# Layer 1 of a two-layer convolutional attention: one shift in 16 goes from VectorE to GpSimd, and the weights of each unit's last two chunks are summed by TensorE

## The chip, the cores and the metric

The kernel runs on one core of a Trainium2 chip. A core has TensorE (PE; its weight loads are listed as PEld), VectorE (DVE), ScalarE (ACT), GpSimd (POOL) and SyncE (SP, which issues most DMAs). Each works through its own queue in order and waits on semaphores for the others. The metric is the device time of one launch in microseconds, the median of the runs; the times of single instructions come from one profiled execution.

## The reference, cut to what matters

`x` is 2 x 256 x 64 x 64, so two images of 256 channels and N = 4096 places. Layer 0 is an attention with four heads of 16 channels and is not touched here. Layer 1 is an attention with four heads of 64 channels:

```python
def _L1_conv_ref(x, w_qkv, b_qkv, w_out, b_out):
    ...
    qkv = jnp.einsum('oc,bchw->bohw', w_qkv, x) + b_qkv[None, :, None, None]
    qkv = qkv.reshape(b, HEADS, 3 * head_dim, h * w)
    q, k, v = jnp.split(qkv, 3, axis=2)
    scale = 1.0 / jnp.sqrt(jnp.asarray(head_dim, x.dtype))
    attn = jax.nn.softmax(jnp.einsum('bhdn,bhdm->bhnm', q, k) * scale, axis=-1)
    out = jnp.einsum('bhnm,bhdm->bhnd', attn, v).reshape(b, c, h, w)
    return jnp.einsum('oc,bchw->bohw', w_out, out) + b_out[None, :, None, None] + x
```

All is in 32-bit floats. Each softmax needs, for a query, the maximum over 4096 keys, the exps of the shifted scores, their sum, and their product with v.

## The kernel before

**Units, chunks and groups.** Layer 1 is cut into 32 units: an image, a pair of heads, and 512 queries. A unit's 4096 keys are 32 chunks of 128 (`NM`), and a chunk's tile is 128 keys x (2 heads x 512 queries), 128x1024. The chunks form two groups of 16 (`GS`, `NG`), each with a maximum of its own; the groups are put together at the end by a factor.

**What happens to a chunk.** `score` makes the scores on TensorE (L876) in PSUM; two buffers, `pair`, take turns. `keep` takes them into the group's running maximum on VectorE (L893), then copies them to SBUF on ScalarE (L894) as the tile `raw`, from a ring of 26. When a group has all its scores, `turn_max` transposes the maxima (L906), `fold` reduces them to one negated maximum a query (L923) and sends them through DRAM, so that they come back as `row`, the same values in all 128 partitions (L926, L930). In `row` a head's queries stand in an order in which two neighbours belong to different halves of a block, so it is read with every second element. `place_shift` has ScalarE copy `row`, put in order, into a PSUM tile (L943). Then, chunk by chunk, `shift` adds that to `raw` on VectorE (L951), and `weigh` takes the exp on ScalarE (L963) and has GpSimd add the weights to the group's `acc` (L973 for the first two chunks of a group, L975 for each later one). `gather` multiplies the weights with v on TensorE (L1004).

**Sums.** `acc` has still 128 keys to be added up. `total` does it on TensorE with a matrix of ones (L1026): a result of 32 equal rows for each group and head, at rows 0, 32, 64 and 96 of the PSUM tile `misc`. That tile has one buffer, which the projections of keys, values and queries and all transposes use in turn. `keep_total` copies the sums out on ScalarE (L1034).

**Order.** It is written out by hand: `seq` keeps instructions in program order on each engine. A step handles two chunks, 16 steps make a unit (`US`), and a chunk's shift comes `LAG` = 11 steps after its scores, so the end of a unit overlaps with the next one. Step t has these parts in this order:

- scores of chunks 2t and 2t+1; `weigh` of chunk 2t-23; what is hung at "start" and "early"
- `keep` of 2t, `shift` and `weigh` of 2t-22; what is hung at "early end"
- `keep` of 2t+1, `gather` of 2t-24 and 2t-23; "late" and "late end"; `shift` of 2t-21; "end"

`at(t, place, ...)` hangs the rest between. Counted in a unit's own steps 0 to 15: the maxima are turned in step 8 and, for the second group, in step 0 of the next unit. `place_shift` comes at the end of step 10, and of step 2 of the next unit. The weights of chunks 30 and 31 are gathered in step 11 of the next unit, whose "early" part projects half of the queries of the unit after into `misc`, which ScalarE reads at "early end" (L858). `total` follows in step 12. Chunk 6 of a unit is shifted in its step 14, chunk 22 in step 6 of the next one.

**The last unit.** From chunk `LATE` on, weights are summed on TensorE already in half of the steps (`on_tensor`, `late_sums`, L990), since nothing follows that would cover GpSimd.

Of the kernel before, what the change touches and what calls it, by code (L numbers as in the profile page):

```python
# [10 lines left out]
ALU = mybir.AluOpType  # L11
# [3 lines left out]
P = 128  # L15
# [5 lines left out]
D1 = 64  # L21
# [5 lines left out]
def conv_attention_kernel(  # L27
# [19 lines left out]
    nc = tc.nc  # L47
    B, _, N = x.shape
    NJ = N // NB
    NM = N // P  # L50
# [75 lines left out]
    for s in range(3):  # L126
        t = const_prep.tile([P, CC, P], F32, tag=f"wpad{s}", name=f"wpad{s}")
# [27 lines left out]
    for i in range(2):  # L155
        t = const0.tile([P, PB, P], F32, tag=f"negmax0_{i}", name=f"negmax0_{i}")
# [20 lines left out]
    def layer1_constants():  # L177

        w1 = const.tile([P, CC, 3, C], F32, tag="w1", name="w1")
        for c in range(CC):  # L180
            for k in range(3):
                later_load(
                    w1[:, c, k, :].rearrange("p (h d) -> p h d", d=D1),
                    w_qkvT[c * P : (c + 1) * P, :].rearrange(
                        "p (h t d) -> p t h d", t=3, d=D1
                    )[:, k],
                )
        wo1 = later_load(
            const.tile([P, CC, C], F32, tag="wo1", name="wo1"), w_outT.rearrange(by_chunk, p=P)
        )  # L190

        b1 = const.tile([P, PR, 3], F32, tag="b1", name="b1")
        for k in range(2):
            later_load(
                b1[k * D1 : (k + 1) * D1],
                b_qkv_col.rearrange("d (g k t) -> d g k t", k=2, t=3)[:, :, k, :],
            )
        b1v = later_load(
            const.tile([P, H, D1], F32, tag="b1v", name="b1v"),
            b_qkv_row.rearrange("(h t d) -> t h d", t=3, d=D1)[2].partition_broadcast(P),  # L200
        )
        bo1 = later_load(const.tile([P, CC], F32, tag="bo1", name="bo1"), b_out)
        ones = const.tile([P, D1], F32, tag="ones", name="ones")
        nc.gpsimd.memset(ones, 1.0)
        return w1, wo1, b1, b1v, bo1, ones


    seq = tc.keep_in_program_order
# [24 lines left out]
    with own0:  # L233
# [189 lines left out]
        def weigh(t, g):  # L423
            u = b, j = units0[t // NM]
            m = t % NM
            pt = l0w.tile([P, 2, NB], F32, tag="p", bufs=4, name=f"p0_{b}_{j}_{m}_{g}")
            for k in range(2):
                h = 2 * g + k
                r = slice(32 * h, 32 * h + 32)

                late = 4 * (t + LEAD0 - END0) + h
                if late >= 0 and late % 7 < 4:
                    ps = bank(f"s0_{b}_{j}_{m}_{h}")
                else:
                    ps = ps2.tile([P, NB], F32, tag="s", name=f"s0_{b}_{j}_{m}_{h}")
                seq(nc.tensor.matmul(  # L436
                    ps, kTs[b][r, bass.ts(m, P)], qs0[u][r, :], start=True, stop=True
                ))
                seq(nc.scalar.activation(pt[:, k, :], ps, AF.Exp, scale=D0**-0.5))  # L439
            pts[t, g] = pt  # L440
# [205 lines left out]
        w1, wo1, b1, b1v, bo1, ones = layer1_constants()  # L646
# [4 lines left out]
        def misc(name):  # L651
            return small_bank[0](name)
# [57 lines left out]
        for i in range(NJ):  # L710
            k = (0, 0, i)
# [17 lines left out]
        for t in range(-LEAD0 + NM, max(t for t, _ in extras) + 1):  # L729
            ahead = t + LEAD0  # L730
            whole = ahead >= END0
            hung(t, "start")
            if 0 <= t < END0:
                weigh(t, 0)
            if ahead < END0:
                maxima(ahead, 1)
            if 0 <= t - 1 < END0 and not whole:
                gather(t - 1, 0)
            hung(t, "middle")
            if 0 <= t < END0:  # L740
                weigh(t, 1)
            if ahead < END0:
                maxima(ahead, 0)
            if 0 <= t - 1 < END0:
                gather(t - 1, None if whole else 1)
            hung(t, "end")
# [12 lines left out]
    units = [(b, g, j) for b in range(B) for g in range(PR) for j in range(NJ)]  # L759
    GS = NM // 2  # L760
    NG = NM // GS
# [2 lines left out]
    END = len(units) * US  # L764


    LATE = len(units) * NM - 2 * LAG
    with (
        tc.tile_pool(name="l1", bufs=2) as l1,
# [7 lines left out]
        rmax, negs, rows_in, shifts, raws, accs = {}, {}, {}, {}, {}, {}  # L777
        avs1, srows, losts, joined, halves = {}, {}, {}, {}, {}
# [160 lines left out]
        def place_shift(u, n):  # L939
            b, g, j = u  # L940
            ps = psb.tile([P, 2, NB], F32, tag="shift", name=f"shift_{b}_{g}_{j}_{n}")
            row = rows_in.pop((u, n))
            seq(nc.scalar.copy(  # L943
                ps.rearrange("p k (a i m) -> p (k a) i m", m=P, i=2),
                row.rearrange("p k (a m i) -> p (k a) i m", m=P, i=2),
            ))
            shifts[u, n] = ps

        def shift(t):
            u = units[t // NM]  # L950
            seq(nc.vector.tensor_tensor(  # L951
                raws[t], raws[t], shifts[u, t % NM // GS], ALU.add
            ))

        def on_tensor(t):
            return t >= LATE and (t // 2 % 2 == 1 or t == 2 * END - 3)

        def weigh(t):
            u = b, g, j = units[t // NM]
            m = t % NM  # L960
            n = m // GS
            p = raws[t]
            seq(nc.scalar.activation(p, p, AF.Exp, scale=D1**-0.5))  # L963

            if on_tensor(t):
                return
            if (u, n) not in first:
                first[u, n] = p
            elif (u, n) not in accs:
                accs[u, n] = l1.tile(  # L970
                    [P, 2, NB], F32, tag="acc", bufs=3, name=f"acc_{b}_{g}_{j}_{n}"
                )
                seq(nc.gpsimd.tensor_tensor(accs[u, n], first[u, n], p, ALU.add))  # L973
            else:
                seq(nc.gpsimd.tensor_tensor(accs[u, n], accs[u, n], p, ALU.add))  # L975

        def late_sums(of):


            if "sums" not in late:  # L980
                late["sums"] = psp.tile([P, 2, NB], F32, tag="pair", name="late_sums")
            t = of[1] if of[1] is not None else of[0]
            u, n = (units[t // NM], t % NM // GS) if t is not None else (units[-1], 0)
            for k in range(2):
                for i in range(2):
                    if of[i] is None and (i == 1 or n == 1 and t != 2 * END - 3):
                        continue
                    p = raws[of[i]] if of[i] is not None else accs[u, n]
                    r = D1 * i + 32 * k
                    seq(nc.tensor.matmul(  # L990
                        late["sums"][r : r + 32, n, :], ones[:, :32], p[:, k, :],
                        start=(n, r) not in begun, stop=True, skip_group_check=True,
                    ))
                    begun.add((n, r))

        def gather(t):
            u = b, g, j = units[t // NM]
            m = t % NM
            n = m // GS
            if m % GS == 0:  # L1000
                avs1[u, n] = psv.tile([P, NB], F32, tag="av", name=f"av1_{b}_{g}_{j}_{n}")
            v = vs[b, g, m // PB]
            for k in range(2):
                seq(nc.tensor.matmul(  # L1004
                    avs1[u, n][k * D1 : (k + 1) * D1, :], v[:, m % PB, k, :], raws[t][:, k, :],
                    start=(m % GS == 0), stop=(m % GS == GS - 1),
                ))
            if on_tensor(t) and t % 2 == 1 and t != 2 * END - 1:
                late_sums((t - 1, t) if on_tensor(t - 1) else (None, t))
            elif t == 2 * END - 2:  # L1010
                late_sums((t, t + 1))
            raws.pop(t - 2, None)
            if m % GS == GS - 1:
                a = l1.tile([P, NB], F32, tag="avs", name=f"avs1_{b}_{g}_{j}_{n}")
                seq(nc.scalar.copy(a, avs1.pop((u, n))))
                avs1[u, n] = a

        def total(u):


            b, g, j = u
            srows[u] = misc(f"sum1_{b}_{g}_{j}")
            for n in range(NG):
                for k in range(2):
                    r = D1 * n + 32 * k
                    seq(nc.tensor.matmul(  # L1026
                        srows[u][r : r + 32, :], ones[:, :32], accs[u, n][:, k, :],
                        start=True, stop=True,
                    ))

        def keep_total(u):
# [161 lines left out]
        for n, u in enumerate(units):  # L1193
            b, g, j = u
# [231 lines left out]
```

## Time and profile before

| | |
|---|---|
| Median of 3 runs | 4668.57 us (4666.47 to 4668.93) |
| Profiled execution | 4667.5 us |
| Its span | 4665.7 us |
| Granted TensorE clock in it, mean | 0.997 |
| Layer 0, and the change to layer 1 | about the first 2060 us |
| One unit of layer 1, start to start | 79.8 us in units 3 to 23, 79.9 later |

A line of the page's list of groups names the source line, engine and operation, then output<-inputs, the shapes and the count; after the bar come the group's busy time in us and the mean of one in ns, and after the second bar how long the engine stood idle before such instructions, and what ended that. A line of a timeline gives the start, the length (several equal instructions in a row are merged, x8), and in brackets an idle time before it. Durations of neighbours overlap a little: VectorE's operations on 128x1024 last 1.21 us but start 1.13 us apart. A TensorE matmul of 32-bit floats appears as two passes, so that the four matmuls of `gather` are x8.

### The profile page before, as it was taken

The page shows a single profiled execution, that of the slowest core. Times are in us where ns is not written, and L with a number is a line of the kernel's source. Part 1 is how long each engine was busy: PE and PEld are TensorE (multiplying, and loading weights), DVE is VectorE, ACT ScalarE, POOL GpSimd, SP SyncE. Part 2 cuts the span into 40 slices and gives each one's busy share as a digit, 9 for nine tenths or more (in the row PEclk, how much of TensorE's full clock was granted, in tenths as well). Part 3 has the DMA queues.
Part 4 walks back from the last instruction along what each step waited for, and adds up shares of the span by engine and source line. Part 5 has one row for each costly group of instructions (what it writes and reads, how often), then busy time and mean ns, then how long its engine had stood idle before and what let it go on. Part 6 is the DMA issues. An engine that isn't in the chain of part 4 may idle for free. (4 is left out here: it accounts for less than half of the span.)

```text
span 4665.7 us, 70910 instructions
## 1 busy us (share of the span) xinstructions
PE 4496.5 (96%) x27290; PEld 1511.0 (32%) x27290; DVE 3894.2 (83%) x4506; ACT 3429.5 (74%) x4588; POOL 2513.9 (54%) x1306
## 2 busy tenths in 40 slices
PE   8999999999999999999999999999999999999998
PEld 3433333333333333332333333333333333222232
DVE  6777777777777777439999999999999999999997
ACT  3366666666666666668888888888888888888885
POOL 5300000000000000009999999999999999999995
PEclk9999999999999999999999999999999999999999
DMA  3100000000000000121111221111211112121213
GB/s 100 39 4 20 20 20 15 15 15 15 15 17 15 15 13 13 40 77 35 35 37 33 63 48 42 35 37 43 69 41 39 37 33 62 48 53 37 53 39 111
DMA packets 199682, 174.70 MB, mean 37 GB/s; under 512 B 121256, under 2 KB 122088, under 8 KB 199344
## 3 DMA queue, kind: packets, MB, share of 16 engines
q1 hardware_dynamic: 197488, 169.58, 13.9%
q8 instruction: 214, 3.51, 0.3%
q14 instruction: 124, 1.02, 0.1%
q10 hardware_dynamic: 1856, 0.59, 0.1%
HBM read 127.65 MB, written 42.48 MB: 36 GB/s over the span
## 5 line engine op out<-in xcount | busy, mean ns | idle before, releaser
L975 POOL TENSOR_TENSOR acc<-acc,raw 128x1024 f32<-128x1024 f32 x883 | 2095.2, 2373 | 82.3 <-ACT raw L963 21.1
L402 DVE TENSOR_REDUCE mx<-a 128x1 f32<-128x512 f32 x2048 | 1314.4, 685 | 449.7 <-PE a L398 448.7
L439 ACT ACTIVATE p<-s 128x512 f32<-128x512 f32 x2048 | 1107.8, 595 | 702.1 <-PE a L398 369.3
L876 PE MATMUL s<-q,k 64*128 64x512 f32 x4096 | 1120.9, 637 | 126.1 <-ACT raw L894 117.9
L951 DVE TENSOR_TENSOR raw<-raw,shift 128x1024 f32<-128x1024 f32 x1024 | 1234.2, 1209 | 3.9 <-ACT shift L943 2.6
L893 DVE TENSOR_TENSOR rmax<-s,rmax 128x1024 f32<-128x1024 f32 x960 | 1168.7, 1217 | 74.4 <-PE s L876 68.3
L436 PE MATMUL s<-q,kT 32*128 32x512 f32 x4096 | 1218.0, 640 | 0.0
L894 ACT COPY raw<-s 128x1024 f32<-128x1024 f32 x1024 | 1034.2, 1010 | 207.3 <-DVE rmax L893 162.0
L963 ACT ACTIVATE raw<-raw 128x1024 f32<-128x1024 f32 x1024 | 1084.8, 1060 | 133.6 <-DVE raw L951 101.2
L398 PE MATMUL a<-kT,q 32*128 32x512 f32 x4096 | 1129.3, 643 | 1.4 <-DVE mx L402 1.3
L1004 PE MATMUL av<-raw,v 128*64 128x512 f32 x4096 | 992.8, 605 | 3.5 <-ACT raw L963 3.4
L451 PE MATMUL av<-p,v 128*32 128x256 f32 (+1 forms) x7904 | 650.1, 399 | 0.6 <-ACT avs L465 0.6
L876 PEld LDWEIGHTS s<-q,k 64*128 64x128 f32 x4096 | 314.6, 185 | 858.5 <-ACT raw L894 600.9
L501 POOL TENSOR_TENSOR f<-f,dyn 128x16 f32<-128x16 f32 x15 | 3.3, 221 | 1027.3 <-DVE f L500 1027.3
L436 PEld LDWEIGHTS s<-q,kT 32*128 32x128 f32 x4096 | 397.2, 183 | 425.8 <-issue 392.6
L451 PEld LDWEIGHTS av<-p,v 128*32 128x32 f32 x7904 | 157.7, 108 | 751.4 <-issue 737.1
L1004 PEld LDWEIGHTS av<-raw,v 128*64 128x64 f32 x4096 | 247.7, 136 | 468.8 <-issue 350.1
L552 POOL TENSOR_SCALAR res<-res 128x1024 f32<-128x1024 f32 x16 | 16.7, 1045 | 659.6 <-ACT res L551 659.6
L398 PEld LDWEIGHTS a<-kT,q 32*128 32x128 f32 x4096 | 305.1, 183 | 31.5 <-DVE mx L402 18.2
L973 POOL TENSOR_TENSOR acc<-raw,raw 128x1024 f32<-128x1024 f32 x64 | 152.6, 2385 | 124.2 <-ACT raw L963 124.2
L923 DVE TENSOR_REDUCE negs<-rt 128x4 f32<-128x512 f32 x126 | 86.7, 688 | 50.4 <-PE rt L906 50.4
L306 DVE RECIPROCAL std<-std 128x128 f32<-128x128 f32 x64 | 56.1, 920 | 39.5 <-ACT std L301 39.5
(335 smaller groups left out, 1835.1 us busy)
## 6 DMA issues: line engine op xcount, KB each, us to landing
row<-neg SPq DMA_DIRECT2D x128, 256.0 KB
x<-in_x_dram SPq DMA_DIRECT2D x16, 512.0 KB
res<-in_x_dram SPq DMA_DIRECT2D x16, 512.0 KB
x<-res SPq DMA_DIRECT2D x16, 512.0 KB
att<-rows SPq DMA_DIRECT2D x62, 128.0 KB
kd<-k1s SPq DMA_DIRECT2D x24, 256.0 KB
vd<-v1s SPq DMA_DIRECT2D x24, 256.0 KB
k<-kd SPq DMA_DIRECT2D x24, 256.0 KB
```

Source lines behind the costliest of these rows:

```text
L398: seq(nc.tensor.matmul(ps, qs0[u][r, bass.ts(i, P)], kTs[b][r, bass.ts(m, NB)], start=True, stop=True,))
L402: seq(nc.vector.tensor_reduce(mxs[u][:, i * H + h, m : m + 1], ps, AX.X, ALU.max))
L436: seq(nc.tensor.matmul(ps, kTs[b][r, bass.ts(m, P)], qs0[u][r, :], start=True, stop=True))
L439: seq(nc.scalar.activation(pt[:, k, :], ps, AF.Exp, scale=D0**-0.5))
L451: seq(nc.tensor.matmul(avs[u][32 * h : 32 * h + 32, cols], vs0[b][:, m, 32 * h : 32 * h + 32], pts[t, h // 2][:, h % 2, cols], start=(m == ...
L876: seq(nc.tensor.matmul(ps[:, k, :], ks[b, g, m // PB][r, bass.ts(m % PB, P)], qs1[u][r, :], start=True, stop=True,))
L893: seq(nc.vector.tensor_tensor(rmax[u, n], ps, before, ALU.max))
L894: seq(nc.scalar.copy(raw, ps))
L951: seq(nc.vector.tensor_tensor(raws[t], raws[t], shifts[u, t % NM // GS], ALU.add))
L963: seq(nc.scalar.activation(p, p, AF.Exp, scale=D1**-0.5))
L975: seq(nc.gpsimd.tensor_tensor(accs[u, n], accs[u, n], p, ALU.add))
L1004: seq(nc.tensor.matmul(avs1[u, n][k * D1 : (k + 1) * D1, :], v[:, m % PB, k, :], raws[t][:, k, :], start=(m % GS == 0), stop=(m % GS == GS ...
```

## The change

One chunk of each group, the one with the number 6 in it (chunks 6 and 22 of a unit), is shifted by GpSimd instead of VectorE. GpSimd reads `row` itself, with every second element, since the ordered copy is in PSUM; the addition stands in GpSimd's queue where `place_shift` is called, four steps before the chunk's turn. The last group of the last unit is left out. In exchange GpSimd no longer adds chunks 30 and 31 of a unit to `acc` (except in the last unit, where TensorE has these already). Their sums are made on TensorE from the weights themselves, right behind their `gather`, and land in rows 64 to 127 of the tile that `total` completes a step later; so `misc` is taken one step earlier, and `total` adds the second group's `acc` to what is there.

```diff
+    ALSO = 6
...
             shifts[u, n] = ps
+            if (u, n) != (units[-1], NG - 1):
+                a = raws[units.index(u) * NM + n * GS + ALSO]
+                seq(nc.gpsimd.tensor_tensor(
+                    a.rearrange("p k (a i m) -> p (k a) i m", m=P, i=2),
+                    a.rearrange("p k (a i m) -> p (k a) i m", m=P, i=2),
+                    row.rearrange("p k (a m i) -> p (k a) i m", m=P, i=2),
+                    ALU.add,
+                ))
 
         def shift(t):
             u = units[t // NM]
+            if t % GS == ALSO and t < (len(units) - 1) * NM + GS:
+                return
             seq(nc.vector.tensor_tensor(
                 raws[t], raws[t], shifts[u, t % NM // GS], ALU.add
             ))
...
-            if on_tensor(t):
+            if on_tensor(t) or m >= NM - 2:
                 return
...
                 late_sums((t, t + 1))
+            if m == NM - 1 and u != units[-1]:
+                srows[u] = misc(f"sum1_{b}_{g}_{j}")
+                for i in (t - 1, t):
+                    for k in range(2):
+                        r = D1 * (NG - 1) + 32 * k
+                        seq(nc.tensor.matmul(
+                            srows[u][r : r + 32, :], ones[:, :32], raws[i][:, k, :],
+                            start=(i < t), stop=False, skip_group_check=True,
+                        ))
...
             b, g, j = u
-            srows[u] = misc(f"sum1_{b}_{g}_{j}")
             for n in range(NG):
                 for k in range(2):
                     r = D1 * n + 32 * k
                     seq(nc.tensor.matmul(
                         srows[u][r : r + 32, :], ones[:, :32], accs[u, n][:, k, :],
-                        start=True, stop=True,
+                        start=(n < NG - 1), stop=True, skip_group_check=True,
                     ))
```

## The prediction

> **What bounds the kernel now.** The change lies in layer 1, the second half of the span, so I read the page's totals and costliest groups first.
>
> ```profile
> PE 4496.5 (96%) x27290; PEld 1511.0 (32%) x27290; DVE 3894.2 (83%) x4506; ACT 3429.5 (74%) x4588; POOL 2513.9 (54%) x1306
> L975 POOL TENSOR_TENSOR acc<-acc,raw 128x1024 f32<-128x1024 f32 x883 | 2095.2, 2373 | 82.3 <-ACT raw L963 21.1
> L951 DVE TENSOR_TENSOR raw<-raw,shift 128x1024 f32<-128x1024 f32 x1024 | 1234.2, 1209 | 3.9 <-ACT shift L943 2.6
> L893 DVE TENSOR_TENSOR rmax<-s,rmax 128x1024 f32<-128x1024 f32 x960 | 1168.7, 1217 | 74.4 <-PE s L876 68.3
> L943 ACT COPY shift<-row 128x1024 f32<-128x1024 f32 x64 | 71.2, 1113 | 3.8 <-DMA row<-neg 1.5
> ```
>
> These shares mix two layers. One unit of layer 1 repeats every 79.8 us, and the table by stretches shows one such period:
>
> ```profile
> 2974.80:3054.60 79.80, 75.73 (x324) 24.77 (x322) 75.98 (x71) 69.51 (x76) 74.23 (x37) 1.00 0.17 37
> ```
>
> After the length come PE, PEld, DVE, ACT and POOL. PE, DVE and POOL are each busy 93 to 95%, so totals don't say which sets the pace; each place of the change has to be read. First the waits from 2200 to 4600 us (sum, times, longest):
>
> ```profile
> DVE rmax L893 <- PE s L876: 62.3, 149, 0.9
> PE s L876 <- ACT raw L894: 105.3, 211, 0.9
> POOL acc L973 <- ACT raw L963: 74.9, 60, 2.1
> ```
>
> DVE waits for scores; PE waits for a score buffer that ACT empties. Now PE's timeline around the place where the new matmuls go (step 11 of the following unit: the av x8 at 2973.84 are chunks 30 and 31, the sums at 2978.02 are step 12):
>
> ```profile
> 2972.78 1.13 PE L806 MATMUL q1p<-b_('q', (0, 1, 4))_24637,w 128*128 128x256 f32 x4
> 2973.84 1.94 PE L1004 MATMUL av<-raw,v 128*64 128x512 f32 x8
> 2975.71 2.38 PE L876 MATMUL s<-q,k 64*128 64x512 f32 x8
> 2978.02 1.07 PE L1026 MATMUL sum<-acc,ones 128*32 128x512 f32 x8
> 2979.02 1.94 PE L1004 MATMUL av<-raw,v 128*64 128x512 f32 x8
> 2988.39 1.94 PE L1004 MATMUL av<-raw,v 128*64 128x512 f32 x8
> 2990.26 2.28 PE L876 MATMUL s<-q,k 64*128 64x512 f32 x8
> ```
>
> From 2970.74 to past 2992 each PE group starts as the one before ends. DVE in the same stretch, and at step 6:
>
> ```profile
> 2976.89 1.22 DVE L893 TENSOR_TENSOR rmax<-s,rmax 128x1024 f32<-128x1024 f32 x1 [0.36 <-PE s L876]
> 2987.79 1.21 DVE L951 TENSOR_TENSOR raw<-raw,shift 128x1024 f32<-128x1024 f32 x1
> 2991.43 1.22 DVE L893 TENSOR_TENSOR rmax<-s,rmax 128x1024 f32<-128x1024 f32 x1
> 3031.74 1.22 DVE L893 TENSOR_TENSOR rmax<-s,rmax 128x1024 f32<-128x1024 f32 x1 [0.58 <-PE s L876]
> ```
>
> DVE waits for PE there, not PE for DVE. Last, ACT's read of the bank that the new sums need, and POOL where the second group's shift goes in:
>
> ```profile
> 2975.55 0.47 ACT L858 ACTIVATE q<-q1p,b 128x256 f32<-128x256 f32 x1
> 3010.71 7.28 POOL L975 TENSOR_TENSOR acc<-acc,raw 128x1024 f32<-128x1024 f32 x3
> 3018.75 2.39 POOL L973 TENSOR_TENSOR acc<-raw,raw 128x1024 f32<-128x1024 f32 x1 [0.77 <-ACT raw L963]
> ```
>
> **PE, added: 31 units, 4 matmuls (8 traced passes) each.** They follow the av of step 11, where the next group could start at 2975.71. They write the misc bank, which has one buffer, and ACT reads the queries out of it until 2975.55+0.47=2976.02; the wait is about 0.3 us. The passes use two of the array's column ranges (rows 64 and 96 of the result), four passes each. Two rows price that: av, also 8 passes on two ranges, 2973.84 to 2975.71, 1.87; the present sums, 8 passes on four ranges, 2978.02 to 2979.02, so 2 passes a range in 1.00 and 4 in 2.00. I take 1.94. Against it: the two score chunks of step 12 start 1.25 apart where back to back is 1.06, a wait for a buffer that will be over, 0.19. Part of that comes back, because the later chunk's copy and the next scores are late by the full amount. Net 2.05 to 2.25, taken 2.15 us a unit; 31 x 2.15 = 66.7 us.
>
> The Trainium skill (TensorEngine Tiling (Array Packing), Theoretical Speedup) gives up to 4x for a small dimension of at most 32, which would make the 8 passes 1.00 us and the sum some 29 us less. The trace shows that speed where four ranges are written; two are written here.
>
> Does anything downstream take the delay in? From 2976 to 2992 PE has only one other gap, about 0.1 before chunk 29, and it waits for a copy that is late too. The larger gaps after (0.61 at 2996.07, the two around L1051 and L876 up to 0.57) end with DVE or ACT work that follows these very scores. I count nothing back.
>
> **DVE, removed: 63 shifts.** Their spacing is 1.13 (2987.79 to 2988.91), so 71.2 us of DVE. Chunk 6 is the one at 2987.79, in step 14. Without it, the maximum of chunk 29 moves up by about 1.0, then the next shift; but the maximum of chunk 30 at 2991.43 needs scores that PE begins at 2990.26 behind its av of 2988.39, and that order doesn't move. Chunk 22 is at 3027.69, in step 6; the following maximum at 3031.74 already waits 0.58 for PE, which runs without a gap from 3026.99 to 3036.12. Both cuts lengthen a DVE wait: 0. If that cover were gone, each would give up to 1.13.
>
> **POOL, swapped: 62 additions out, 63 shifts in.** Out: 62 x 2.373 = 147.1. In: no row of POOL at this size reads every second element, as the shift does of `row`. Below: the plain 2.373 (149.5 in all). Nothing makes it cheaper, since it has the elements of an addition. Above: ACT's copy of the same `row` takes 1113 against 1010 ns plain, 1.10 times, so 2.61 (164.6). Far end, an estimate: if POOL pays for the stretch that it reads, one of its two inputs counts double, 1.5 x 2.373 = 3.56. I take 2.4, the same operation with one input changed, with ACT's row as the nearest sign of a surcharge. The Trainium skill (GPSIMD Engine Reference, Performance pitfalls for Q7 kernels) puts 50% on reads with a step of more than 8 bytes; this step is 8 bytes, so the rule lets the plain price hold. No row here shows it.
>
> Place of the first group's shift: behind chunk 29's addition, ahead of the next group's first, before which POOL idles 2.1 us and where an addition of chunks 30 and 31 each has gone. It costs nothing, even if a row comes late. Place of the second: between the additions of chunks 14 and 15. Chunk 14's ends about 3015.5, the shift runs to 3018.0, chunk 15's to 3020.4 (before: 3017.99), then chunks 16 and 17 start 1.6 late. Queued behind chunk 15's addition is a buffer: ACT's copy of chunk 9 of the next unit, at 3020.67, goes into the slot that it frees. The margin is 0.3 at 2.373 and nil at 2.61. Beyond that each 0.1 costs up to 0.1 a unit. Later additions had 3 to 5 us to their slot's reuse and keep 1.4 or more; the two dropped ones at the unit's end give the 1.6 back. `row` is landed: ACT read it from 3012.38 on, and of 64 reads two waited. The two exps that now wait for POOL come four steps after. SP's next write of `row`, 6 steps on, now waits for POOL too, 20 us past its read. 0 us.
>
> **Sum.** The profiled execution is 4667.5 us (span 4665.7 and 1.8 around it), 1.1 under the median of 4668.57. 4667.5+66.7 = 4734.2; on the median's footing 4735.
>
> **Rivals.** (A) PE pays, and a cut shift counts: if one of the two lay on the path, 31 x 1.13 = 35 back, 4700; if the passes overlapped as the present sums do, 1.00 for 8 and not 1.94, 31 x 0.94 = 29 less, 4706. Against: the waits named above. Chance 0.09. (B) Faster: the period is DVE's. It's busy 76.0 of 79.8, PE has 4.1 idle to take 2.15 in, and the 71.2 count: 4597. For: DVE has the largest sum. It decides if PE's recorded ends are late enough that PE has over 2 us of true slack in steps 11 to 14; against: the maxima start within 0.05 of the scores' recorded ends. Chance 0.08; that both count in full (-4.5, 4664, no change) 0.03. (C) The strided shift outgrows POOL's margin: at the far end of 3.56, chunk 15's addition ends 1.2 later than with 2.373, 0.9 past the margin, and ACT's copy with it; with 0.2 for POOL's later start 31 x 1.1 = 34 more, 4769. For: the copy at 3020.67 is followed at once by the scores that need its buffer. Against: ACT's own surcharge is 0.1. Chance 0.12. The forecast, 4730 to 4740 by its own terms, 0.68. That the swap isn't made is excluded by the program's order: POOL has one 128x1024 operation more.
>
> **Numbers.** Range 4700 to 4770: it takes in A and C's bounds, and leaves B and no change out. About 0.2% (9 us) is what a measurement tells from no change. Faster 0.08, same 0.03, slower 0.89.
>
> **What would show it.** Right: period near 82.0; new matmuls 1.9 behind an 0.3 wait on L858; DVE's wait for scores (62.3) grown by over 100; shifts on POOL near 2.4, ACT's copies not waiting on POOL. Wrong: a period of 77 to 80, PE's waits for ACT shrunk; or copies released by POOL.

## The result and the profile after

The changed kernel takes 4721.89 us (4721.34 to 4722.56, 4 runs) beside 4668.19 for the kernel before: 1.0116 times, 95% interval 1.0098 to 1.0133, or 53.7 us more where 66.7 were forecast. It is inside the range, on the side that was forecast, and a fifth smaller than the sum; it lies under the 4730 to 4740 that the forecast gave by its own terms.

The profiled execution has a span of 4719.6 us. One period of layer 1 in the table by stretches (length, then PE, PEld, DVE, ACT and POOL busy):

```profile
2934.80:3016.40 81.60, 77.20 (x330) 25.26 (x328) 73.98 (x69) 69.12 (x76) 74.08 (x37) 1.00 0.16 36
```

The period grew from 79.8 to 81.6 us. PE gained 1.5 us of work, DVE lost 2.0 and POOL lost 0.15; which of these moved the time, the steps below and the runs tell. The waits from 2200 to 4600 us:

```profile
DVE rmax L896 <- PE s L879: 170.4, 234, 2.7
PE s L879 <- ACT raw L897: 110.5, 263, 0.9
PE sum L1030 <- ACT q L861: 7.6, 29, 0.3
```

DVE's wait for scores went from 62.3 to 170.4 us. That holds both what was cut from DVE and the longer period: with the new sums alone (the first run below) it is 125.8.

One row of these waits looks like the sign that the prediction named for being wrong: ACT's copies of scores are put down to POOL's small operation on `sums` (L1138), 29 times, 16.4 us. But that copy starts 1.31 us after the start of its own maximum on DVE (3006.38 to 3007.69), just as the copies next to it do (3001.43 to 3002.74, 3010.80 to 3012.11), so by this spacing it is the maximum that releases it. And the row is the same, 29 times and 16.4 us, in the run where GpSimd shifts nothing, so the moved shift isn't behind it.

PE's timeline around the new matmuls (L1030), for the same unit as before:

```profile
2991.40 1.94 PE L1017 MATMUL av<-raw,v 128*64 128x512 f32 x8
2993.63 1.91 PE L1030 MATMUL sum<-raw,ones 128*32 128x512 f32 x8 [0.29 <-ACT q L861]
2995.47 1.99 PE L879 MATMUL s<-q,k 64*128 64x512 f32 x8
2997.39 1.07 PE L1047 MATMUL sum<-acc,ones 128*32 128x512 f32 x8
2998.38 1.94 PE L1017 MATMUL av<-raw,v 128*64 128x512 f32 x8
3000.25 1.13 PE L879 MATMUL s<-q,k 64*128 64x512 f32 x4
3001.64 1.13 PE L879 MATMUL s<-q,k 64*128 64x512 f32 x4 [0.27 <-ACT raw L897]
```

The wait for the `misc` bank is there, 0.29 us, and the 8 passes take 1.84 us up to the next start. DVE and POOL at the places of the change:

```profile
2996.64 1.23 DVE L896 TENSOR_TENSOR rmax<-s,rmax 128x1024 f32<-128x1024 f32 x1 [2.56 <-PE s L879]
3010.80 1.23 DVE L896 TENSOR_TENSOR rmax<-s,rmax 128x1024 f32<-128x1024 f32 x1 [0.63 <-PE s L879]
```

```profile
2989.67 2.43 POOL L953 TENSOR_TENSOR raw<-raw,row 128x1024 f32<-128x1024 f32 x1
2995.99 2.37 POOL L986 TENSOR_TENSOR acc<-raw,raw 128x1024 f32<-128x1024 f32 x1 [3.90 <-ACT raw L976]
3034.86 2.41 POOL L953 TENSOR_TENSOR raw<-raw,row 128x1024 f32<-128x1024 f32 x1
```

The first group's shift lies in POOL's idle time with 3.9 us to spare, and the shift costs 2.41.

**The same by steps.** The trace gives the start of every score copy on ScalarE; the spacing of the even chunks' copies is the length of a step. Means over seven units in the middle (8 to 14), in us:

```
                     step 1     2     6     9    11    12    13    14   period
before                 5.72  5.34  5.20  4.52  4.53  5.14  4.58  4.79    79.81
changed                5.74  5.33  5.19  4.52  6.70  4.78  4.96  4.42    81.64
```

Steps 0 to 10 are unchanged, step 6 with its cut shift among them. Step 11, with the new matmuls, is 2.17 longer; steps 12 to 14 give 0.36 back, take 0.38 and give 0.37. The net is 1.82 a period. Some periods of before were longer than 79.8 for other waits, so all 31 together grew by 53.3.

### The profile page after: what moved, and what is told of

Same layout as the page of the kernel before. It is cut to its first block, busy times and chain, and to the rows that moved or that the text cites. A ratio compares the mean times of both kernels' runs of the same rounds, so it can differ in the third digit from the quotient of the medians.

```text
span 4719.6 us, 71331 instructions
## 1 busy us (share of the span) xinstructions
PE 4542.9 (96%) x27538; PEld 1526.2 (32%) x27538; DVE 3832.3 (81%) x4443; ACT 3418.6 (72%) x4588; POOL 2512.0 (53%) x1307
## 5 line engine op out<-in xcount | busy, mean ns | idle before, releaser
L988 POOL TENSOR_TENSOR acc<-acc,raw 128x1024 f32<-128x1024 f32 x821 | 1948.0, 2373 | 115.8 <-ACT raw L976 65.2
L879 PE MATMUL s<-q,k 64*128 64x512 f32 x4096 | 1107.7, 634 | 126.5 <-ACT raw L897 124.8
L964 DVE TENSOR_TENSOR raw<-raw,shift 128x1024 f32<-128x1024 f32 x961 | 1159.9, 1211 | 2.8 <-ACT shift L946 1.5
L953 POOL TENSOR_TENSOR raw<-raw,row 128x1024 f32<-128x1024 f32 x63 | 151.8, 2409 | 36.0 <-DMA row<-neg 36.0
```

The lines of the kernel that those rows point to most:

```text
L879: seq(nc.tensor.matmul(ps[:, k, :], ks[b, g, m // PB][r, bass.ts(m % PB, P)], qs1[u][r, :], start=True, stop=True,))
L964: seq(nc.vector.tensor_tensor(raws[t], raws[t], shifts[u, t % NM // GS], ALU.add))
```

## The experiments

The runs were on several chips, on which the kernel before took 4668 to 4681 us; each is compared by its ratio to the kernel before on its own chip. Verdicts rest on ratios and on the step table. Steps that an edit doesn't reach agree to 0.02 us between chips, but for step 2 (more on it below):

```
                     step 1     2     6     9    11    12    13    14   period   last 7
before                 5.72  5.34  5.20  4.52  4.53  5.14  4.58  4.79    79.81    79.88
sums only              5.72  5.72  5.19  4.52  6.70  4.78  4.96  4.59    82.17    82.17
6 and 22 unshifted     5.74  5.68  5.19  4.53  4.53  5.15  4.56  4.81    80.19    80.20
12 and 28 unshifted    5.06  6.15  5.19  3.93  4.57  5.12  4.63  4.74    79.40    79.92
12 and 28 on GpSimd    5.06  6.51  5.19  3.92  6.71  4.78  4.96  4.59    81.86    81.50
changed, again         5.74  5.43  5.19  4.53  6.70  4.78  4.96  4.42    81.74    81.82
four ranges            5.74  5.40  5.19  4.52  5.85  4.78  4.96  4.42    80.87    81.04
28 unshifted           5.72  5.43  5.19  3.92  4.57  5.12  4.64  4.74    79.33    79.90
28 on GpSimd           5.72  5.36  5.19  3.92  4.58  5.12  4.64  4.74    79.27    81.20
28, first 24 units     5.72  5.57  5.19  3.92  4.57  5.11  4.64  4.74    79.45    80.25
```

The last column is the mean period from unit 24 on.

**The sums alone.** The changed kernel without the shift on GpSimd:

```diff
-            if (u, n) != (units[-1], NG - 1):
-                a = raws[units.index(u) * NM + n * GS + ALSO]
-                seq(nc.gpsimd.tensor_tensor(
...
-                ))
...
-            if t % GS == ALSO and t < (len(units) - 1) * NM + GS:
-                return
```

> VectorE shifts every chunk again; GpSimd still drops the additions of chunks 30 and 31 and TensorE makes their sums. Theory (the cut shifts are worth nothing, the sums on TensorE's path are the whole loss): the time of the changed kernel, 4717 to 4727 us. Rival (a cut shift gave back part, and what is seen is a net): the recovery of about 0.35 us a unit seen in step 14 is the cut's, 31 x 0.35 = 11 more, 4733; if a whole shift counted, 31 x 1.13 = 35 more, 4757.

It takes 1.0126 times the kernel before (1.0111 to 1.0141), 61.3 us more. Beside the changed kernel's 1.0115 and 1.0116 that leaves 0.1%, some 5 us, for the shift on GpSimd; the intervals of the ratios overlap, but the step table shows where it lies: step 14 is 4.59 here and 4.42 in the changed kernel, in each unit, 31 x 0.17 = 5.3. So neither answer was right as put: the sums cost 1.99 us a unit (steps 11 to 14 together 21.03 against 19.04), and the cut in step 14 pays 0.17 of it back. The reason is in ScalarE's queue. In the run with the sums alone, VectorE's shift of chunk 6 ends at 3098.26, and only then can ScalarE take its exp (first line). The copy of chunk 29 stands behind that exp, and TensorE waits 0.40 for it before the scores of chunk 31 (second line):

```profile
3098.29 1.06 ACT L966 ACTIVATE raw<-raw 128x1024 f32<-128x1024 f32 x1
3100.67 1.13 PE L879 MATMUL s<-q,k 64*128 64x512 f32 x4 [0.40 <-ACT raw L897]
```

In the changed kernel the exp starts 0.91 after the copy of chunk 28 does, instead of 1.07, and the same scores wait 0.23:

```profile
3010.98 1.13 PE L879 MATMUL s<-q,k 64*128 64x512 f32 x4 [0.23 <-ACT raw L897]
```

**No one shifts chunks 6 and 22.** Kernel before, with

```diff
         def shift(t):
             u = units[t // NM]
+            if t % GS == 6 and t < (len(units) - 1) * NM + GS:
+                return
```

> The kernel before, but nobody shifts chunks 6 and 22 of a unit (they stay unshifted, the last group apart); sums as before. Theory (VectorE waits for TensorE in steps 6 and 14): 4664 to 4670, no change. Rival (VectorE sets the period): 63 x 1.13 = 71 less, 4597; half of it, 4633.

It takes 4681.44 us beside 4681.27: 0.9997 (0.9987 to 1.0006). 71 us of VectorE's work were taken away with nothing in exchange, and the time didn't move; by the interval it fell by 6 us at most. The work turned into waiting:

```profile
DVE rmax L893 <- PE s L876: 125.1, 208, 1.2
```

That is 62.8 us more than the 62.3 of before (in a profile from another chip), about as much as was cut in that stretch.

**No one shifts chunks 12 and 28.** The same with `t % GS == 12`; the cuts then lie in steps 1 and 9.

> The kernel before, but nobody shifts chunks 12 and 28 of a unit, whose turns are steps 1 and 9. In the trace of before VectorE runs there without a wait from the second reduction of the turned maxima on for some 11 to 20 us, while TensorE idles 0.4 to 0.8 us at a time. Theory (what a cut shift is worth hangs on its place, not on VectorE's total): a third to the whole of 63 x 1.13 = 71 less, 4597 to 4645. Rival (VectorE has slack everywhere, the period is TensorE's and ScalarE's): 4668.

It takes 0.9960 times the kernel before (0.9945 to 0.9975), 17.6 us less: the place does decide, but it is a quarter of 71, under the third that was expected. Step 9 is 0.6 shorter, 3.93 against 4.52. Step 1 is 0.66 shorter as well, but step 2 is longer than in the run before it, on the same chip, by 0.47. ScalarE's waits, first of the run with chunks 6 and 22 unshifted, then of this one:

```profile
ACT shift L943 <- DMA row<-neg: 13.9, 22, 1.1
```

```profile
ACT shift L943 <- DMA row<-neg: 29.9, 27, 1.9
```

At the end of step 2 ScalarE copies `row`, which has come through DRAM from the maxima reduced in step 0. What step 1 saves brings ScalarE to that copy before the row is there.

**GpSimd shifts chunks 12 and 28.** The changed kernel with `ALSO = 12`.

> The changed kernel with the chunk that GpSimd shifts moved from 6 to 12 in its group; all else the same. Theory of the place: 4722 less what cutting chunks 12 and 28 is worth, 4650 to 4699, if GpSimd's addition keeps up. Rival (no place helps, the sums cost alone decides): 4722.

It takes 1.0084 times the kernel before (1.0069 to 1.0099) where the change has 1.0115: about 15 us better, still 41 slower than before. So the place counts, but the theory missed: it wanted 23 to 72 off the changed kernel. Step 9 gains 0.6, step 14 loses its 0.17, step 2 waits more. The sums' cost stays.

**The changed kernel again**, as the measure on the next runs' chip.

> The changed kernel itself, beside the others on their chip, as the measure for them. All theories: 1.0116 of the kernel before. It also shows the value of the cut shifts as the difference from the run with the sums alone (1.0126): 0.1%, 5 us, by the theory that a cut in step 14 is worth 0.17 us a unit.

It takes 1.0115 times the kernel before (1.0100 to 1.0130), 4727.67 us. The first result repeats on another chip.

**Four column ranges.** The changed kernel with

```diff
-                        r = D1 * (NG - 1) + 32 * k
+                        r = D1 * (i < t) + 32 * k
...
-                            start=(i < t), stop=False, skip_group_check=True,
+                            start=True, stop=False, skip_group_check=True,
```

> The changed kernel, but the sums of chunk 31 go to rows 0 and 32 of the result and those of chunk 30 to rows 64 and 96, so that the 8 passes use four column ranges (chunk 31 is then lost from the sums, since total starts rows 0 and 32 anew). Theory (the price of the new sums is four passes one after the other in each of two ranges): 8 passes in 1.0 instead of 1.84 us, 31 x 0.84 = 26 less than the changed kernel. Rival (the passes are bound by their count, or by the wait for the bank alone): the same as the changed kernel.

It takes 4700.83 us, 1.0057 times the kernel before (1.0042 to 1.0072): 26.8 less than the changed kernel, as expected to within a microsecond. In this run's timeline:

```profile
2987.50 1.06 PE L1030 MATMUL sum<-raw,ones 128*32 128x512 f32 x8 [0.29 <-ACT q L861]
2988.49 1.99 PE L879 MATMUL s<-q,k 64*128 64x512 f32 x8
```

The same 8 passes take 0.99 instead of 1.84 to the next start, the wait before them is unchanged, and step 11 shrinks from 6.70 to 5.85. What is taken from PE there is taken from the period, which falls by 0.87. The edit also ends the accumulation of chunk 31 on the rows of chunk 30. That isn't what sped the passes up: `total` in the changed kernel accumulates on rows 64 and 96, over four ranges in all, and its 8 passes take 0.99 (2997.39 to 2998.38), against 1.00 without accumulation before.

**No one shifts chunk 28.** Kernel before, with `t % NM == GS + 12`, so the cut in step 9 alone.

> The kernel before, but nobody shifts chunk 28 of a unit (chunk 12 is shifted again). Theory (the cut in step 9 is worth 0.6 us a unit, and the one in step 1 is lost again in step 2 to the wait for the row that comes back through DRAM): as with both chunks cut, 31 x 0.6 = 18.6 less than before, 0.996. Rival (both cuts are worth the same): half, 9 less, 0.998.

It takes 4659.35 us beside 4673.8: 0.9968 (0.9957 to 0.9980), 14.5 us less, with 9.3 to 20.1 for the interval. The 18.6 of the theory lies inside it, the rival's 9 at its edge, so the time alone doesn't decide. The table speaks for most of the theory: step 9 has the whole gain here, and in the run that cut both chunks, step 2 took back 0.47 of the 0.68 of step 1 (beside the run before it, on the same chip), so that some 0.2 stayed. The periods of the two runs, 79.33 and 79.40, come from chips on which step 2 differs and don't decide it. In the last seven units the period doesn't shrink (79.90), though step 9 does; step 12 is 0.5 longer there, 5.55 where the kernel before has 5.08. TensorE's part of `total` in such a unit, and its weight loads for the second group's half, show why:

```profile
4406.71 1.64 PE L1028 MATMUL sum<-acc,ones 128*32 128x512 f32 x8
4407.30 0.14 PEld L1028 LDWEIGHTS sum<-acc,ones 128*32 128x32 f32 x4 [0.44 <-POOL acc L977]
```

To the next start, at 4408.28, it takes 1.57, against 1.00 in the kernel before (4416.20 to 4417.20). GpSimd also adds the output in those eight units, its last addition to `acc` ends at 4407.24, and the 0.6 us saved by the others is enough for `total` to reach an `acc` that isn't finished. Seven units without the 0.6 are 4 us, which accounts for 14.5 instead of 18.6.

**GpSimd shifts chunk 28 and gives nothing away.** Kernel before, with the shift on GpSimd for that chunk, and no sums on TensorE:

```diff
+            if n == NG - 1 and u != units[-1]:
+                a = raws[units.index(u) * NM + GS + 12]
+                seq(nc.gpsimd.tensor_tensor(
...
+                ))
...
         def shift(t):
             u = units[t // NM]
+            if t % NM == GS + 12 and t < (len(units) - 1) * NM:
+                return
```

> The kernel before, but GpSimd shifts chunk 28 of a unit and still adds all weights; nothing new on TensorE. Theory: VectorE's cut in step 9 is kept, GpSimd takes 2.4 us a unit into its idle time (74.2 of 79.8 busy before) and ends chunk 31 just before total needs it: 10 to 19 less than before, 0.996 to 0.998. Rival (GpSimd's later end holds total or a buffer up): 1.6 us a unit too late at most, so up to 31 more than before.

It takes 0.9991 times the kernel before (0.9982 to 1.0001), 3.5 us less and not clear of zero. Up to unit 23 the theory holds, with a mean period of 79.3 in the middle and 79.5 over all of them; in the last seven the period is 81.2. There GpSimd has the additions for the output too, and its last addition of a unit ends after TensorE wants the sum:

```profile
4415.04 1.05 PE L1036 MATMUL sum<-acc,ones 128*32 128x512 f32 x4
4417.04 1.05 PE L1036 MATMUL sum<-acc,ones 128*32 128x512 f32 x4 [0.94 <-POOL acc L985]
```

The two halves of `total` stand together in the kernel before. Here the second waits for `acc`, and longer than in the run without the shift: 2.98 from the first start to the next group's at 4418.02, where that run has 1.57.

**The same in the first 24 units only.** Against the run before:

```diff
-            if n == NG - 1 and u != units[-1]:
+            if n == NG - 1 and u in units[:-NJ]:
...
-            if t % NM == GS + 12 and t < (len(units) - 1) * NM:
+            if t % NM == GS + 12 and t < (len(units) - NJ) * NM:
```

> The kernel before, with GpSimd shifting chunk 28 in the first 24 units alone; in the last 8, where GpSimd has the output additions too (76.5 of 79.8 busy before) and held total up by 1.9 us a unit, VectorE does it again. Theory: the gain of 0.55 us in each of 24 units is kept and the loss of 1.3 in the last 8 is gone: 13 less than before, 0.997. Rival (what GpSimd puts off in 24 units comes due in the 25th): 0.998 to 1.000.

It takes 4660.81 us beside 4675.12: 0.9971 (0.9960 to 0.9982). It is faster than both kernels, and 14 us faster than the one before, as the theory had it. The rival comes due once: chunk 28 of the 24th unit is shifted in the 25th, where the output's additions begin, and step 12 is 6.67 there against about 5.09 in the units after. Nothing on TensorE was needed for it.

## Why the prediction was right, and where its sum was off

- **What sets the pace in steps 11 to 14: right.** PE's path took the new work nearly whole; four ranges instead of two gave back 26.8 us. Rival B, that the period is VectorE's, falls for the places of the change with the run that took 63 shifts away for nothing; in step 9 a cut shift is worth 0.6.
- **The terms of the sum.** The wait for the bank was 0.29 (0.3 forecast), the passes 1.84 (1.94); counted from 2993.27, where the next group could have started, the two make 2.20. The gap between the two score chunks of step 12 was mis-sized: I subtracted 0.19, and 0.39 closed. From the first score to the sums it was 2975.71 to 2978.02, 2.31; it is 2995.47 to 2997.39, 1.92. My 1.06 for back to back is the time from the second chunk's start to the next group (2.31 - 1.25); without a wait, the second chunk starts 0.86 after the first (1.99 - 1.13), and 1.25 - 0.86 is 0.39.
- **"Part of that comes back".** It did: chunk 27's scores follow chunk 26's by 1.39 (3000.25 to 3001.64), held by a copy that is late in full. But I stopped there, and the same 0.36 was saved again two groups later: scores and projection of step 14 start 2.29 apart before (2985.47 to 2987.76) and 1.93 after:

```profile
3005.20 2.00 PE L879 MATMUL s<-q,k 64*128 64x512 f32 x8
3007.13 0.70 PE L809 MATMUL q1p<-b_('q', (0, 1, 4))_24657,w 128*128 128x256 f32 x2
```

  I had named that gap "about 0.1" and said its copy would be late too. It was late by 1.8, PE by 2.17, so PE found it done. That is the step that was wrong, "I count nothing back": 2.20 - 0.39 + 0.36 - 0.36 is 1.81, near the 1.82 of the changed kernel. The sums' net cost by themselves was 1.99 instead of 2.15, under the 2.05 that I had as the least.
- **The cut shifts: 0 forecast, 0.17 a unit measured.** Step 6 gave nothing, as read from DVE's wait of 0.58. In step 14 I followed VectorE alone; the 0.17 came through ScalarE's exp. Taken alone, without the sums, the cuts gave nothing at all. With 1.99 - 0.17 = 1.82, what is missing from the forecast of 2.15 is explained. My 0 had the right cause for step 6 and missed a path in step 14.
- **GpSimd: right.** 2.41 for the strided shift, where I had taken 2.4 out of 2.37 to 3.56; no surcharge of the kind that rival C needed. The Trainium skill (GPSIMD Engine Reference, Performance pitfalls for Q7 kernels) has it that an 8-byte step is not yet beyond the limit, and this row agrees. The copy of chunk 9, for which a margin of 0.3 was left, didn't come later: step 4 is 4.78 in both traces. (Of the 64 reads of `row` by ACT, three waited in the trace of before, 1.5 us in all; the two that I gave are those from 2200 to 4600 us.)
- **Rival A** had a part of the truth, a cut that counts, at 0.17 instead of 1.13.

## What to carry to other kernels

Three engines at 93 to 95% don't share a bound: each step has its own. Before moving work from one engine to another, find in the timeline who waits for whom at the very steps where it leaves and where it lands; the cheapest test is a run that leaves the work out. And follow a delay through every later gap: a gap that ends with something late by less than the delay closes.

## What the runs showed of the hardware that was not expected

The way of `row` through DRAM takes different times on different chips. The same changed kernel spent nothing on ScalarE's wait for `row` between 2200 and 4600 us in its first profile, and 6.3 us on the second chip, with step 2 at 5.33 and 5.43 and medians of 4721.89 and 4727.67 us. On a third chip the run with chunks 6 and 22 unshifted spent 13.9 us on it, and the kernel before took 4681 us there. SyncE's own wait for the first of the two transfers, the maxima on their way to DRAM, shows it whatever the kernel: between 2200 and 4600 us it is 2.5 us on average in both profiles of the first comparison, 2.64 to 2.69 in the four of the second chip, 2.74 to 2.80 in the four of the third, and 2.67 in the one profile from a fourth. Why the chips differ isn't shown. How much of these differences the wait makes wasn't tried.
